# A value product moved in front of the last tile of an output projection, in a gated attention and feed-forward block

## The chip, the cores and the metric

The kernel runs on one core of one Trainium2 chip. The metric is the device time of one execution in microseconds. A core has five engines that run side by side, each through its own instructions in their order: PE (TensorE, matrix products; its weight loads are shown apart as PEld), DVE (VectorE), ACT (ScalarE), POOL (GpSimd) and SP (SyncE, which here issues almost all DMAs). Engines wait for one another by semaphores.

## The reference

There are 32 sequences of 64 tokens with 512 features, as queries (`x`) and as context (`ctx_4096`), 32 heads of width 128, and after the attention a linear layer with adapters (LoRA):

```python
q = (layernorm(x) @ Wq).reshape(b, 64, 32, 128)          # b = 32
k = (ctx @ Wk).reshape(...);  v = (ctx @ Wv).reshape(...)
score = einsum('bqhd,bkhd->bhqk', q, k) / sqrt(128) + position_bias
probs = softmax(where(mask, score, -inf)), 0 where masked
a = einsum('bhqk,bkhd->bqhd', probs, v).reshape(b, 64, 4096) @ Wo
x = x + tanh(g_xattn) * a
y = layernorm(x) @ weight.T + bias + lora(layernorm(x))
out = x + tanh(g_ffn) * y
```

All is float32. The wide products are made as three products of rounded parts: a number is split into a high part (rounded to a type that PE reads at full rate) and a low part (the rest), and high x high, high x low and low x high are summed (`mm3`). So each operand of a wide product must first be split: ACT copies it with rounding (high part), then DVE or POOL subtracts (low part).

## The kernel before

The 2048 tokens are done in two halves of 1024 tokens (`p` = 0, 1), each of which is 8 tiles of 128 tokens (`NT` = 8). A half first makes all keys and values and stores them in HBM (`stage_a`), then runs the attention (`run` within `attention`), by 16 pairs of heads (`NPR` = 16); after the second half the linear layer follows.

For one pair `n` the attention has four kinds of work on PE:
- `q_unit(n)`: the queries of the pair, 42 wide matmuls (128x512).
- `score(n, ...)`: per head 16 small matmuls of queries with keys (each stands twice in the record). Two pairs are scored at a time, 128 matmuls in the record. Behind each of the four score tiles come, on DVE, scale and bias (L863) and the row maximum (L865), then on POOL the subtraction of the maximum (L866), then a beat; ACT's exponential follows.
- `pv(n)`: the product of probabilities with values, 64 small matmuls (128 in the record) into four PSUM banks (`po`, L1010). Each bank is then rounded: ACT copies it into `ch` (L1014), DVE subtracts for `cl` (L1015), and a beat follows. There is one `ch` and one `cl`, used by almost all pairs. At its end `pv(n)` issues the load of the values of the next pair.
- `oproj(n)`: the output projection of the pair, 8 tiles of 6 wide matmuls (`mm3` of `ch`, `cl` and the weight `wo`, high and low), each added to the running sum `acc` by DVE (L1059), with a beat.

The order of PE is written out by hand. From the fifth pair on the loop of `run` goes in cycles of two pairs:

```python
for a in range(4, NPR, 2):
    oproj(a - 3)
    q_unit(a)
    start_o(a - 2)
    pv(a - 2)
    q_unit(a + 1)
    if a < NPR - 2:
        oproj(a - 2)
    start_o(a - 1)
    if a < NPR - 2:
        pv(a - 1)
    ...
    score(a, a + 1)
```

Side work is kept in a list of generators, `streams`. A call of `beat()` advances every one of them by one step, in the order of the list, and the step's instructions go to the queues of their engines at that point. `drain` runs one to its end. Among the side streams: the making of query weights (`prep`, 8 steps on ACT and POOL), the turning of probabilities (`turned`, with ACT copies L896), the bias and mask (`bias_mask`, POOL L815), and the rounding of the output weight.

That last one is `prep_o(n)`, which `start_o(n)` puts into the list. Its first step rounds one half of `wo` (ACT copies the high part, L90; POOL subtracts for the low part, L91), its second step the other half, its third issues the fetch of the next raw `wo` on SP (L259). It writes the one buffer that the projection before it has read. `oproj(n)` takes it from there; within a tile of `mm3` the first matmul reads high half 0 of `wo`, the second low half 0, the third high half 0, the fourth high half 1, the fifth low half 1, the sixth high half 1.

PSUM has eight banks, taken in turn: a projection takes 8, a value product 4, two pairs of scores 4.

## Time and profile before

| | |
|---|---|
| Median of 3 runs | 1477.29 us (1476.85 to 1477.81) |
| Profiled execution | 1477.5 us, of which 1475.7 us from the first to the last instruction (span) |
| PE | 1467.0 us busy, 99% |
| POOL | 1052.0 us, 71% |
| DVE | 940.2 us, 64% |
| ACT | 714.6 us, 48% |
| Mean granted clock of PE | 1.000 |
| Projection, wide matmuls with `ch` (L100) | 896, 278.2 us |
| Value product `po` (L1010) | 3840, 63.4 us |
| Scores `ps` (L861) | 2048, 65.2 us |
| Low half of `wo` on POOL (L91) | 56, mean 1299 ns |
| Score subtraction on POOL (L866) | 64, mean 1050 ns |

How to read it: busy times of different engines overlap and don't add up to the span. Matmuls are pipelined, their durations overlap too, so the distance from start to start counts: six wide matmuls take 1.36 us. In the chain of work that ended last PE has 97%. A line of a timeline gives the start, the duration of a group, engine, line, operation with its output and inputs, the count, and in brackets the idle time before it and what ended it.

### The profile page before, as it was taken

Reading aid. Unit: us, or ns where it says so; the run is one execution under the profiler, and the core shown is the slowest. Engines: PE = TensorE matmul, PEld = TensorE weight load, DVE = VectorE, ACT = ScalarE, POOL = GpSimd, SP = SyncE. Lnnn points to the kernel's source line nnn. Section 1 sums busy time; section 2 is a strip of 40 time slices with the busy share of each in tenths; the row PEclk is TensorE's granted clock in tenths of the full one; section 3 lists DMA queues with packets and bytes.
Section 4 is the critical chain, followed back from the end, with each engine's and each line's share of the span. In section 5 each row is a group of like instructions: output and inputs, shape, how many; then the busy total and the mean of one; then the engine's idle time right before and its main releaser. Section 6 shows DMA issues by size and latency. Waiting matters only on the chain.

```text
span 1475.7 us, 31292 instructions
## 1 busy us (share of the span) xinstructions
PE 1467.0 (99%) x12008; PEld 1220.4 (83%) x12008; DVE 940.2 (64%) x1589; ACT 714.6 (48%) x1582; POOL 1052.0 (71%) x1160
## 2 busy tenths in 40 slices
PE   9999999999999999999999999999999999999999
PEld 7888888888888888888888888888888888888887
DVE  5675464367675677576479756435767567757774
ACT  5444233346555665666334423334655665566611
POOL 4999378969767676767989938896875758577520
PEclk9999999999999999999999999999999999999999
DMA  5754554475443455353385765437545344625554
GB/s 194 287 204 164 179 179 174 143 261 185 152 168 106 168 180 208 101 186 109 127 294 203 235 226 186 173 136 260 184 152 178 103 170 170 217 93 184 136 127 131
DMA packets 148343, 259.38 MB, mean 176 GB/s; under 512 B 44417, under 2 KB 78209, under 8 KB 144098
## 3 DMA queue, kind: packets, MB, share of 16 engines
q1 hardware_dynamic: 147906, 256.87, 50.7%
q8 instruction: 94, 1.54, 0.4%
q10 hardware_dynamic: 288, 0.52, 0.1%
q14 instruction: 55, 0.45, 0.1%
HBM read 179.74 MB, written 77.61 MB: 174 GB/s over the span
## 4 chain that ended last, share of the span: by engine, by line
PE 97%; DVE 1%; issue 1%; ACT 1%; POOL 0%; DMA 0%; SPq 0%; DVEq 0%; POOLq 0%
PE pa L100 23%; PE pxq L100 6%; PE pvq L100 6%; PE pvv L100 6%; PE pxv L100 6%; PE pzv L100 6%; PE pzq L100 6%; PE pzk L100 6%; PE pvk L100 6%; PE pxk L100 6%; PE po L1010 4%; PE ps L861 4%; PE pf L100 3%; PE pyq L100 3%; PE pyv L100 3%; PE pyk L100 3%
## 5 line engine op out<-in xcount | busy, mean ns | idle before, releaser
L100 PE MATMUL pa<-wo,ch 128*128 128x512 f32 x896 | 278.2, 392 | 0.4 <-ACT ch L1014 0.4
L896 ACT COPY pt<-tp 32x256 f32<-32x256 f32 x452 | 182.4, 404 | 69.7 <-DVE tp L899 60.1
L100 PEld LDWEIGHTS pa<-wo,ch 128*128 128x128 f32 x896 | 166.6, 188 | 36.0 <-ACT ch L1014 0.7
L100 PE MATMUL pa<-wo,cl 128*128 128x512 f32 x448 | 174.1, 389 | 0.0
L1059 DVE TENSOR_TENSOR acc<-pa,acc 128x512 f32<-128x512 f32 x192 | 129.4, 681 | 53.5 <-PE pa L100 53.5
L815 POOL TENSOR_TENSOR sm<-sm,madd 128x512 f32<-128x512 f32 x60 | 77.2, 1295 | 96.5 <-DMA sm<-bias 96.5
L888 POOL TENSOR_TENSOR sm<-sm,r 128x512 f32<-128x512 f32 x64 | 66.8, 1044 | 72.5 <-DVE r L887 70.2
L351 DVE TENSOR_TENSOR vt<-pvv,vt 128x512 f32<-128x512 f32 x64 | 44.2, 691 | 103.1 <-PE pvv L100 103.1
L1015 DVE TENSOR_TENSOR cl<-po,ch 128x512 fp32r<-128x512 f32 x112 | 74.5, 689 | 47.6 <-ACT ch L1014 47.2
L100 PEld LDWEIGHTS pa<-wo,cl 128*128 128x128 f32 x448 | 84.1, 188 | 17.7
L866 POOL TENSOR_TENSOR sm<-sm,mx 128x512 f32<-128x512 f32 x64 | 67.0, 1050 | 34.9 <-DVE mx L865 34.7
L351 DVE TENSOR_TENSOR qT<-pvq,qT 128x512 f32<-128x512 f32 x64 | 44.1, 690 | 61.9 <-PE pvq L100 60.5
L373 ACT COPY vt<-pxv 128x512 f32<-128x512 f32 x32 | 18.8, 588 | 130.9 <-PE pxv L100 130.9
L875 ACT ACTIVATE sm<-sm 128x512 f32<-128x512 f32 x62 | 39.2, 633 | 78.0 <-POOL sm L866 78.0
L351 DVE TENSOR_TENSOR kT<-pvk,kT 128x512 f32<-128x512 f32 x60 | 41.1, 684 | 54.8 <-PE pvk L100 53.9
L91 POOL TENSOR_TENSOR wo<-rawo,wo 128x512 fp32r<-128x512 f32 x56 | 71.4, 1299 | 3.1 <-ACT wo L90 3.1
L1010 PEld LDWEIGHTS po<-pt,v 64*64 64x64 f32 x3840 | 59.2, 135 | 10.8 <-issue 9.3
L187 POOL TENSOR_TENSOR vs<-wvr,wvr 128x512 f32<-128x512 f32 x24 | 32.1, 1348 | 49.3 <-DMA wvr<-wv 49.3
L861 PE MATMUL ps<-kB,qT 128*64 128x64 f32 x2048 | 65.2, 223 | 2.1 <-issue 2.0
L1014 ACT CAST ch<-po 128x512 fp32r<-128x512 f32 x112 | 63.0, 594 | 7.9 <-PE po L1010 7.8
L861 PEld LDWEIGHTS ps<-kB,qT 128*64 128x64 f32 x2048 | 61.9, 138 | 5.8 <-issue 4.2
L351 DVE TENSOR_TENSOR vt<-pzv,vt 128x512 f32<-128x512 f32 x64 | 44.2, 690 | 34.0 <-PE pzv L100 33.6
(999 smaller groups left out, 3899.2 us busy)
## 6 DMA issues: line engine op xcount, KB each, us to landing
kd<-kT SPq DMA_DIRECT2D x64, 512.0 KB, 3.8
vd<-vt SPq DMA_DIRECT2D x128, 256.0 KB, 2.4
kB<-kd SPq DMA_DIRECT2D x32, 1024.0 KB, 10.6
v<-vd SPq DMA_DIRECT2D x32, 1024.0 KB, 8.0
rawq<-wq SPq DMA_DIRECT2D x32, 512.0 KB, 3.7
sm<-bias SPq DMA_DIRECT2D x64, 256.0 KB, 5.4
rawo<-wo SPq DMA_DIRECT2D x32, 512.0 KB, 3.7
rawk<-wk SPq DMA_DIRECT2D x31, 512.0 KB, 5.3
```

The source lines that it names most:

```text
L91: eng.tensor_tensor(lo, raw, hi.bitcast(F32), ALU.subtract)
L100: nc.tensor.matmul(ps, a, b, start=start and i == 0, stop=stop and i == len(todo) - 1, skip_group_check=True)
L351: nc.vector.tensor_tensor(o, ps, i, ALU.add)
L815: nc.gpsimd.tensor_tensor(t, t, masks[p][0], ALU.add)
L861: nc.tensor.matmul(ps[h * S:(h + 1) * S, t, :], qT[:, i, tok], kT[:, i, tok], start=True, stop=True)
L866: nc.gpsimd.tensor_tensor(s, s, mx.unsqueeze(2).to_broadcast([P, NT, S]), ALU.subtract)
L888: nc.gpsimd.tensor_tensor(t, t, r.unsqueeze(2).to_broadcast([P, NT, S]), ALU.mult)
L896: f(pts[n == NPR - 2][dst, i, :, qi * 32:(qi + 1) * 32], of[src, :, ki * 32:(ki + 1) * 32])
L1010: nc.tensor.matmul(ps[h][d:d + S, k, :], v[keys, t, i * P + d:i * P + d + S], pt[keys, i, t, :], start=True, stop=True)
L1014: nc.scalar.copy(o, ps[h])
L1015: nc.vector.tensor_tensor(l, ps[h], o.bitcast(F32), ALU.subtract)
L1059: nc.vector.tensor_tensor(acc[t], ps, acc[t], ALU.add)
```

## The change

In the cycles with a < NPR - 2 (a = 4, 6, 8, 10, 12, in both halves) the matmuls of `pv(a - 1)` are issued before the last tile of `oproj(a - 2)` instead of after it. Since the last tile still reads `ch` and `cl`, the four roundings of the product, each with its beat, are collected in a list and issued behind that tile. `start_o(a - 1)`, which stood between the projection and the product, now stands behind the roundings. The other calls of `pv` and `oproj` are as before.

```diff
-        def pv(n, cs=(0, 1)):
+        def pv(n, cs=(0, 1), later=None):
             drain(b["s", n])
...
                 for h in range(2):
                     o, l = [x[:, i].rearrange("p (t h s) -> p h t s", h=2, s=S)[:, h, ts[0]:ts[-1] + 1] for x in (hi, lo)]
-                    nc.scalar.copy(o, ps[h])
-                    nc.vector.tensor_tensor(l, ps[h], o.bitcast(F32), ALU.subtract)
-                    beat()
+
+                    def rounded(o=o, l=l, ps=ps[h]):
+                        nc.scalar.copy(o, ps)
+                        nc.vector.tensor_tensor(l, ps, o.bitcast(F32), ALU.subtract)
+                        beat()
+                    if later is None:
+                        rounded()
+                    else:
+                        later.append(rounded)
...
-        def oproj(n, ts=range(NT)):
+        def oproj(n, ts=range(NT), between=None):
             drain(ob.get(n))
             for t in ts:
+                if between and t == NT - 1:
+                    between()
                 ps = psum(f"pa{p}_{n}_{t}")
...
                 if a < NPR - 2:
-                    oproj(a - 2)
+                    later = []
+                    oproj(a - 2, between=lambda: pv(a - 1, later=later))
+                    for x in later:
+                        x()
                 start_o(a - 1)
-                if a < NPR - 2:
-                    pv(a - 1)
-                else:
+                if a == NPR - 2:
                     drain(b["s", a - 1])
                     next(ob[a - 1])
                     held = list(streams)
```

## The prediction

> **What bounds the kernel now.** I read the page's busy shares first, then the waits of PE (TensorE), then the order of time around the moved work, engine by engine.

> ```profile
> PE 1467.0 (99%) x12008; PEld 1220.4 (83%) x12008; DVE 940.2 (64%) x1589; ACT 714.6 (48%) x1582; POOL 1052.0 (71%) x1160
> ```

> PE is idle for 1475.7 - 1467.0 = 8.7 us in all. Its waits by name add up to about 5 us:

> ```profile
> PE ps L861 <- issue: 2.0, 4, 0.8
> PE warm L514 <- POOL ident masks.py:199: 1.3, 1, 1.3
> PE pa L100 <- DVE cx L1015: 1.1, 2, 0.8
> ```

> So no rearrangement can save more than 8.7 us (0.6%), while anything PE must newly wait for is paid in full. The question is what PE's order needs from the other engines after the move. The timelines of PE, DVE, ACT and POOL at the first of the ten changed places (a = 4, first half) answer it. Columns: start us, duration us, engine, line, operation.

> ```profile
> 418.92 0.39 PE L100 MATMUL pa<-wo,cl 128*128 128x512 f32 x1
> 419.23 2.13 PE L1010 MATMUL po<-pt,v 64*64 64x64 f32 x128
> 421.29 3.95 PE L861 MATMUL ps<-kB,qT 128*64 128x64 f32 x128
> 425.17 0.73 PE L100 MATMUL pa<-wo,ch 128*128 128x512 f32 x2
> 425.74 0.40 PE L100 MATMUL pa<-wo,cl 128*128 128x512 f32 x1
> 425.98 0.62 PE L100 MATMUL pa<-wo,ch 128*128 128x512 f32 x2
> ```
> ```profile
> 419.34 0.69 DVE L1059 TENSOR_TENSOR acc<-pa,acc 128x512 f32<-128x512 f32 x1 [0.67 <-PE pa L100]
> ...
> 423.12 1.29 DVE L1015 TENSOR_TENSOR cl<-po,ch 128x512 fp32r<-128x512 f32 x2 [0.31 <-ACT ch L1014]
> 424.32 0.68 DVE L863 SCALAR_TENSOR_TENSOR sm<-ps,sm 128x512 f32<-128x512 f32 x1
> 425.04 0.69 DVE L865 TENSOR_REDUCE mx<-sm 128x8 f32<-128x512 f32 x1
> 425.64 0.68 DVE L863 SCALAR_TENSOR_TENSOR sm<-ps,sm 128x512 f32<-128x512 f32 x1
> ```
> ```profile
> 422.50 0.74 POOL L294 TENSOR_TENSOR wq6p<-wsq,wq6p 128x256 fp32r<-128x256 f32 x1
> 423.19 2.53 POOL L91 TENSOR_TENSOR wo<-rawo,wo 128x512 fp32r<-128x512 f32 x2
> 425.80 1.04 POOL L866 TENSOR_TENSOR sm<-sm,mx 128x512 f32<-128x512 f32 x1
> 427.12 1.05 POOL L866 TENSOR_TENSOR sm<-sm,mx 128x512 f32<-128x512 f32 x1 [0.28 <-DVE mx L865]
> ```

> See POOL. The two low halves of the next output weight (L91, wo) run before the first score's subtraction (L866), and end at 425.72. The projection that reads them starts at 425.17: its second matmul (about 425.50) takes low half 0, its fifth (425.98 + 0.23 = 426.21) low half 1. The slack today is 0.5 us.

> **The change part by part, at this place; ten such places (a = 4, 6, 8, 10, 12 in two halves).**

> *PE order.* Nothing is added; tile 7 of the projection changes places with the value product. A tile repeats every 1.36 us, so the product starts at 419.23 - 1.36 = 417.87. Before a wide product it takes 2.03 (the other product of the cycle, 360.30 to 362.33). The first six wide matmuls behind it take 1.49 instead of 1.36 (362.33 to 363.82), and the step from wide matmuls to scores costs 0.09 more than wide to wide (370.62 to 372.07 = 1.45). Scores then start at 417.87 + 2.03 + 1.49 + 0.09 = 421.48, 0.19 later than now, and the next projection could start at 425.36.

> *Operands of the product, earlier by 1.36 us.* Values: issued at 402.65, landing at most 10.9 us later (slowest of 32), so 413.5. Probabilities: last turned copy on ACT at about 409.9. Both in time: 0. PSUM: the four product banks are held over tile 7, but the fourth score is the first to reuse one, at about 424.4, and that is read out by 422.9: 0.

> *Roundings.* All four pairs come behind tile 7, because tile 7 reads the very ch and cl that they overwrite. DVE first has tile 7's add, at 421.58 (scores start + 0.1) instead of 419.34, then four subtractions at a pitch of 0.60 (1.29 - 0.69): 422.18 to 423.98, then the first score's operation at 424.58, 0.26 later than now. ACT's four copies at a pitch of 0.49 (two in 1.08, one 0.59) stay ahead of that. cl is complete by 424.7, before 425.36: hidden under the scores, 0.

> *The weight rounding, which moves without being named.* The call that queues the rounding of wo as a side stream (start_o) stood before the value product, whose four beats issued both halves and the next fetch. Now it stands behind the four delayed roundings, so the four beats of the scores issue it. A beat comes after each score's POOL subtraction. POOL's queue becomes: subtraction 0, low half 0, subtraction 1, low half 1, subtractions 2 and 3. Subtraction 0 cannot start before DVE has the first row maximum: 1.48 after the score's first DVE operation (424.32 to 425.80; at another place 1126.67 to 1128.15, with POOL idle before it), so 424.58 + 1.48 = 426.06. One subtraction holds POOL 1.09 (two in 2.13, one 1.04), one half 1.24 (2.53 - 1.29):
> - low half 0: 427.15 to 428.44 (1.29 long)
> - subtraction 1: later of 424.58 + 1.32 + 1.48 = 427.38 (score pitch 425.64 - 424.32) and 427.15 + 1.24 = 428.39
> - low half 1: 429.48 to 430.77

> The high halves (ACT, 0.62 each) run right behind the ch copies and before the exponentials; ready by 424.8: 0.

> PE's second matmul therefore waits from about 425.69 to 428.44 (2.75 us), three more run, and the fifth, due at 425.36 + 1.04 = 426.40, waits to 430.77. Late: 4.37 us. With the 0.19 of reordering 4.56 per place, 45.6 in ten.

> *DMAs.* SP's queue gets the fetch of the following wo behind low half 1 instead of at 425.75, about 5 us later, and two key loads behind it (426.91 now); PE itself is 4.5 later, and these are read 20 and 49 us on: 0. The value load no longer stands behind that fetch; nobody waits for it.

> *Given back.* The score stage has gaps of issue at three of the ten places (0.37, 0.68, 0.77) and is longer by 0.26 and 0.23 at two (4.21, 4.18 against 3.95). A gap in the scores is now hidden, since low half 1 ends last: -2.3.

> *Sum.* 45.6 - 2.3 = 43.3 on the profiled execution's 1477.5 us: 1520.8. That execution stands 0.2 over the median of the three runs (1477.29), so 1521 either way.

> *Bounds.* Whether a wait is for half a tile or all of it: at the second place the projection starts at 475.09 while POOL's two halves last until 475.92, so it is by halves; if by the whole tile, PE waits with its first matmul and loses the 1.04 of overlap, +10 in all. Restart of PE after a wait: none to one weight load (0.19) at two waits, 0 to +4; I take 0, since the rows of PEld lie beside matmuls: a weight can be loaded while the matmul waits. DVE's rounding chain 0.3 shorter or longer: -3 to +3.

> *The clock.* A new wait of 2.75 us has no like in the running kernel; the longest is 1.3, at the start. The end of the trace has one:

> ```profile
> 1472.00:1473.00 1.00, 0.52 (x5) 0.31 (x3) 0.44 (x1) 0.00 (x0) 0.00 (x0) 1.00 0.39 131
> ...
> 1475.30:1475.70 0.40, 0.00 (x0) 0.00 (x0) 0.00 (x0) 0.00 (x0) 0.00 (x0) 0.59 0.00 0
> ```

> The seventh number is the granted clock. PE's last matmul ends at 1472.52 and the clock is down 2.8 to 3.2 us later. So the wait is just at the edge. Bounds: nothing, or half speed for some 2.8 us at all ten, 1.4 each, +14. I take nothing, as PE works 0.7 us between its two waits.

> [...]

> **The rivals.**
> 1. *No stall (0.05): 1477.* If the weight rounding still came ahead of subtraction 0, PE would lose only 0.19 x 10 = 1.9, and 2.3 of gaps might close. For it: POOL's backlog ends at 423.19, with 2.9 us free until 426.06, room for both halves. Against: the beats are where they are, and POOL's rows follow the order of issue.
> 2. *Half a stall (0.09): 1498.* One beat falls between, so low half 0 is ahead of subtraction 0 and low half 1 behind it, ready at 427.15 + 1.29 = 428.44: 2.04 late, 2.23 a place, 22.3 - 2.3 = +20.
> 3. *Faster (0.03): 1474.* Today 256 small matmuls follow each other and the sequencer falls behind; a wide tile between them lets it catch up. It decides from both low halves being ready before 426.40, and needs 0.5 us a place, which the issue gaps (2.0 us in all) do not hold.
> 4. *The clock drops too (0.13): 1530 to 1540,* with the wait for the whole tile in the same region.

> **How the numbers follow.** Forecast 0.70: 1521, by its own bounds 1515 to 1531. Rivals 1 and 3 are left out below (0.08), and part of rival 2; above, rival 4 up to 1538. Range 1503 to 1538. A measurement of this kernel tells about 0.2% (3 us) from no change. Faster 0.03; within 0.2% 0.05 (rival 1); slower 0.92.

> **What would show it.** PE busy stays near 1467 and its idle grows by some 43 us, put down to POOL wo L91, twenty waits of about 2.7 and 1.6 us at ten places. POOL's order reads L866, L91, L866, L91. The product starts one tile earlier with no wait; the first score's DVE operation comes about 3.1 us after the scores start. Wrong if POOL shows both L91 before L866 (rival 1), if PE waits for ch or cl, or if the granted clock falls below 1.00 in these stretches.

## The result and the profile after

The changed kernel takes 1540.95 us (median of four runs, 1539.90 to 1541.78), the kernel before beside it 1477.07 us: a ratio of 1.0427, interval 1.0415 to 1.0439, +63.9 us. It is slower, as forecast, but 3 us above the top of the range (1538), and the loss is 64 us where 44 were forecast. The profiled execution took 1541.78 us with a span of 1540.0 us, against 1477.5 and 1475.7.

First the busy share of PE on the page of the changed kernel, then its waits (us in total, times, longest):

```profile
PE 1497.4 (97%) x12008; PEld 1235.4 (80%) x12008; DVE 943.4 (61%) x1589; ACT 714.4 (46%) x1582; POOL 1050.0 (68%) x1160
```
```profile
PE pa L100 <- POOL wo L91: 35.2, 20, 2.5
PE pa L100 <- DVE cx L1017: 1.6, 2, 0.8
```

The new wait is the one forecast: twenty times for the low halves of `wo`, two at each of ten places. But it explains only part of the 64 us, and PE's busy time has grown by 30 us with the same 12008 matmuls. The timelines of POOL and of PE at the first place (a = 4, first half) show both:

```profile
426.58 1.04 POOL L866 TENSOR_TENSOR sm<-sm,mx 128x512 f32<-128x512 f32 x1 [4.30 <-DVE mx L865]
427.58 1.27 POOL L91 TENSOR_TENSOR wo<-rawo,wo 128x512 fp32r<-128x512 f32 x1
428.81 1.05 POOL L866 TENSOR_TENSOR sm<-sm,mx 128x512 f32<-128x512 f32 x1
429.81 1.27 POOL L91 TENSOR_TENSOR wo<-rawo,wo 128x512 fp32r<-128x512 f32 x1
```
```profile
418.36 2.11 PE L1010 MATMUL po<-pt,v 64*64 64x64 f32 x128
420.40 0.73 PE L100 MATMUL pa<-wo,ch 128*128 128x512 f32 x2
...
421.99 3.95 PE L861 MATMUL ps<-kB,qT 128*64 128x64 f32 x128
425.87 0.50 PE L100 MATMUL pa<-wo,ch 128*128 128x512 f32 x1
428.90 0.50 PE L100 MATMUL pa<-wo,ch 128*128 128x512 f32 x1 [2.53 <-POOL wo L91]
429.24 0.40 PE L100 MATMUL pa<-wo,cl 128*128 128x512 f32 x1
429.47 0.40 PE L100 MATMUL pa<-wo,ch 128*128 128x512 f32 x1
431.14 0.79 PE L100 MATMUL pa<-wo,ch 128*128 128x512 f32 x1 [1.27 <-POOL wo L91]
431.73 0.63 PE L100 MATMUL pa<-wo,cl 128*128 128x512 f32 x1
432.15 1.05 PE L100 MATMUL pa<-wo,ch 128*128 128x512 f32 x2
...
437.79 0.39 PE L100 MATMUL pa<-wo,cl 128*128 128x512 f32 x1
438.01 0.61 PE L100 MATMUL pa<-wo,ch 128*128 128x512 f32 x2
438.47 0.39 PE L100 MATMUL pa<-wo,cl 128*128 128x512 f32 x1
```

POOL does subtraction, half, subtraction, half; before the first subtraction it stood idle for 4.30 us, in which both halves (2.53 us in the profile before) would have had room. PE's fifth matmul starts at 431.14 instead of 425.87 + 1.04 = 426.91, 4.23 us late. And then the matmuls are slow: three wide matmuls take 1.28 us (432.15 to 433.43 from group to group), against 0.68 further down (437.79 to 438.47). The table by stretches shows the clock beside it; its columns are the stretch, its length, the busy time of PE, PEld, DVE, ACT, POOL, then the granted clock, the share of the DMA engines and GB/s:

```profile
427.13:430.54 3.41, 0.96 (x3) 0.49 (x3) 3.25 (x5) 1.26 (x2) 3.41 (x4) 1.00 0.02 7
430.54:433.95 3.41, 2.81 (x7) 2.23 (x8) 0.69 (x1) 1.26 (x2) 2.54 (x3) 0.50 0.50 181
433.95:437.36 3.41, 3.41 (x10) 2.64 (x9) 1.65 (x4) 0.00 (x0) 0.54 (x1) 0.50 1.02 429
437.36:440.77 3.41, 3.41 (x17) 2.81 (x16) 3.19 (x7) 0.22 (x1) 1.55 (x2) 1.00 0.38 159
```

The clock of PE is halved from 430.54 to 437.36. In the trace's clock records this happens at all ten places, seven times for 6.83 us and three times for 3.41 us, 58.0 us in all.

The stage sums of the two profiled executions close the account. From the first matmul of the projection to the next query unit the ten places take 174.1 us instead of 110.4 (+63.7); the ten score stages before it take 38.8 instead of 41.9 (-3.1, the gaps of issue are gone); the prediction costed the reordering at +1.9. That is 62.5 of the 64.3 us between the spans.

### The profile page after: what moved, and what is told of

Same layout as the page of the kernel before. It is cut to its first block, busy times and chain, and to the rows that moved or that the text cites. A ratio compares the mean times of both kernels' runs of the same rounds, so it can differ in the third digit from the quotient of the medians.

```text
span 1540.0 us, 31252 instructions
## 1 busy us (share of the span) xinstructions
PE 1497.4 (97%) x12008; PEld 1235.4 (80%) x12008; DVE 943.4 (61%) x1589; ACT 714.4 (46%) x1582; POOL 1050.0 (68%) x1160
## 4 chain that ended last, share of the span: by engine, by line
PE 81%; POOL 9%; issue 5%; DMA 2%; DVE 1%; ACT 1%; POOLq 0%; DVEq 0%
PE pa L100 18%; PE pzv L100 6%; PE pvv L100 6%; PE pxv L100 6%; PE pzk L100 5%; PE pvk L100 5%; PE pxk L100 5%; PE pxq L100 5%; PE pzq L100 5%; PE pvq L100 5%; PE pf L100 3%; PE pyv L100 3%; PE pyk L100 3%; PE pyq L100 2%; POOL wo L91 2%
## 5 line engine op out<-in xcount | busy, mean ns | idle before, releaser
L100 PE MATMUL pa<-wo,ch 128*128 128x512 f32 x896 | 302.2, 416 | 35.6 <-POOL wo L91 35.2
L100 PEld LDWEIGHTS pa<-wo,ch 128*128 128x128 f32 x896 | 177.6, 200 | 83.1 <-POOL wo L91 43.8
L100 PE MATMUL pa<-wo,cl 128*128 128x512 f32 x448 | 182.9, 409 | 0.0
L866 POOL TENSOR_TENSOR sm<-sm,mx 128x512 f32<-128x512 f32 x64 | 66.4, 1044 | 76.6 <-DVE mx L865 76.6
L100 PEld LDWEIGHTS pa<-wo,cl 128*128 128x128 f32 x448 | 90.1, 201 | 18.7
L91 POOL TENSOR_TENSOR wo<-rawo,wo 128x512 fp32r<-128x512 f32 x56 | 71.5, 1291 | 2.8 <-ACT wo L90 2.8
L1010 PEld LDWEIGHTS po<-pt,v 64*64 64x64 f32 x3840 | 59.0, 135 | 10.6 <-issue 9.2
L861 PEld LDWEIGHTS ps<-kB,qT 128*64 128x64 f32 x2048 | 61.2, 138 | 5.9 <-issue 5.1
L351 DVE TENSOR_TENSOR qT<-pzq,qT 128x512 f32<-128x512 f32 x64 | 44.2, 690 | 32.3 <-PE pzq L100 30.7
```

Of the source, the lines that this page charges most:

```text
L91: eng.tensor_tensor(lo, raw, hi.bitcast(F32), ALU.subtract)
L100: nc.tensor.matmul(ps, a, b, start=start and i == 0, stop=stop and i == len(todo) - 1, skip_group_check=True)
L351: nc.vector.tensor_tensor(o, ps, i, ALU.add)
L861: nc.tensor.matmul(ps[h * S:(h + 1) * S, t, :], qT[:, i, tok], kT[:, i, tok], start=True, stop=True)
L866: nc.gpsimd.tensor_tensor(s, s, mx.unsqueeze(2).to_broadcast([P, NT, S]), ALU.subtract)
L1010: nc.tensor.matmul(ps[h][d:d + S, k, :], v[keys, t, i * P + d:i * P + d + S], pt[keys, i, t, :], start=True, stop=True)
```

## The experiments

The theory after this reading, A: the place of `start_o` is the whole cause; it queues the halves of `wo` behind score subtractions, PE waits, and the wait makes the clock fall. The rivals: B, the moved product and its delayed roundings of `ch` and `cl` cost the time; C, the clock falls for a reason other than idle time.

**e1, the weight queued first.** Undoes one part of the change:

```diff
                     oproj(a - 2, between=lambda: pv(a - 1, later=later))
+                    start_o(a - 1)
                     for x in later:
                         x()
-                start_o(a - 1)
+                else:
+                    start_o(a - 1)
```

> The changed kernel with one line moved: start_o(a - 1) stands before the delayed roundings, so their four beats issue the rounding of wo, as before the change; the product stays in front of tile 7. Theory A (the loss comes from the place of start_o alone: both low halves of wo come behind score subtractions on POOL, PE waits some 4.2 us at ten places, and its clock halves after each): no waits for POOL wo, granted clock 1.00 throughout, 1475 to 1480 us. Theory B (the loss comes from the moved product and its delayed roundings of ch and cl): stays near 1541 us.

Measured: 1478.99 us, before 1479.14; ratio 0.9999 (0.9990 to 1.0008). PE no longer waits for `wo`, and its mean granted clock is 1.0 in all eleven runs. On POOL of this kernel the halves are back in front, in the idle time:

```profile
420.15 0.72 POOL L294 TENSOR_TENSOR wq6p<-wsq,wq6p 128x256 fp32r<-128x256 f32 x1
422.68 2.53 POOL L91 TENSOR_TENSOR wo<-rawo,wo 128x512 fp32r<-128x512 f32 x2 [1.80 <-ACT wo L90]
426.81 1.04 POOL L866 TENSOR_TENSOR sm<-sm,mx 128x512 f32<-128x512 f32 x1 [1.61 <-DVE mx L865]
```

So the named part of the change, the product in front of the last tile with its roundings behind, costs and brings nothing that can be measured. All ten score stages here take 3.88 or 3.89 us from their first matmul to the projection's, without the gaps of before. That is 3.1 us less in ten, and the seams of the reordering, costed at 1.9, take most of it back; the rest is within the interval. B falls.

**e2, the weight queued late, nothing else.** The other part alone, on the kernel before:

```diff
-                start_o(a - 1)
                 if a < NPR - 2:
                     pv(a - 1)
-                else:
+                start_o(a - 1)
+                if a == NPR - 2:
```

> The kernel before with one line moved: start_o(a - 1) stands behind pv(a - 1) and its roundings; the product stays behind tile 7. Theory A: POOL's order becomes subtraction, low half, subtraction, low half; PE late by about 3.5 us at ten places (35 us), and 10 to 25 us more if the clock falls: 1510 to 1537 us. Theory B: 1477 us, nothing waits.

Measured: 1521.50 us, ratio 1.0281 (1.0261 to 1.0300). The waits of PE in this kernel, and POOL's order at the first place:

```profile
PE pa L100 <- POOL wo L91: 24.8, 20, 1.7
```
```profile
425.34 1.04 POOL L866 TENSOR_TENSOR sm<-sm,mx 128x512 f32<-128x512 f32 x1 [3.48 <-DVE mx L865]
426.34 1.27 POOL L91 TENSOR_TENSOR wo<-rawo,wo 128x512 fp32r<-128x512 f32 x1
427.57 1.04 POOL L866 TENSOR_TENSOR sm<-sm,mx 128x512 f32<-128x512 f32 x1
428.58 1.27 POOL L91 TENSOR_TENSOR wo<-rawo,wo 128x512 fp32r<-128x512 f32 x1
```

At the first place the fifth matmul starts at 429.89 instead of 426.67, 3.22 late. The clock fell at eight places, 30.7 us in all. A holds: a moved line with no arithmetic of its own makes most of the loss (42 of 64 us). It is less than in the changed kernel: subtraction 0 starts 3.72 us after the scores start (421.62 to 425.34) instead of 4.59 (421.99 to 426.58). That DVE has tile 7's sum and all four roundings still before it there, and here only the later roundings, is the likely reason, but was not tried by itself.

**e3, one half first.** Half of the cause: after the delayed roundings the first step of the rounding of `wo` is issued by hand.

```diff
                 start_o(a - 1)
+                if a < NPR - 2:
+                    next(ob[a - 1])
```

> The changed kernel with the first step of the rounding of wo issued ahead of the scores (one step by hand behind start_o), the second behind the first score subtraction. Theory A: only the fifth matmul waits, for about 2.0 us at ten places: 1496 to 1500 us if the clock holds over a wait of 2 us, 1510 to 1522 us if it falls there too. Theory B: near 1541 us.

Measured: 1503.29 us, ratio 1.0161 (1.0147 to 1.0175), +24.2. One wait is left at each place:

```profile
PE pa L100 <- POOL wo L91: 18.3, 10, 1.8
```

The wait is close to what was expected, 1.83 us for about 2.0; the time lies between the two expected ranges, because the clock neither held nor fell throughout: it fell at three of ten places, for 3.41 us each. A wait of the same 1.83 us left the clock alone at seven places and was followed by a halved clock at three. Here are two stretches of the grid of 3.41 us that e5 describes, each with such a wait; after the first the clock stayed, after the second it fell. PE's busy time, 1.58 us, is the same in both, so these two are not told apart by that number:

```profile
582.56:585.97 3.41, 1.58 (x7) 1.31 (x8) 3.31 (x7) 1.23 (x2) 3.41 (x4) 1.00 0.22 50
633.76:637.17 3.41, 1.58 (x7) 1.01 (x6) 3.31 (x6) 0.83 (x2) 3.41 (x4) 1.00 0.23 42
```

**e4, the wait filled with work.** Takes away the idle time and leaves the lateness. Ahead of `oproj(a - 3)` at the ten places (in the loop's passes with a > 4) stands `fill(a, 11)`:

```diff
+            def fill(a, k):
+                drain(ob.get(a - 3))
+                px = psum(f"fill{p}_{a}")
+                for _ in range(k):
+                    nc.tensor.matmul(px, xq["p1"][0][0][:, 0:P], xq["p1"][0][0], start=True, stop=True,
+                                     skip_group_check=True)
```

> The changed kernel with eleven extra wide matmuls (2.5 us of work whose result nobody reads) ahead of the next projection at each of the ten places, where PE would wait for low half 0. If the halved clock comes from PE's idle time (theory A), the clock stays at 1.00 and more work takes less time: 1513 to 1520 us, with PE still waiting for low half 1 and projection starts at the same distance from the scores. If the clock falls for another reason (rival: the order of small and wide matmuls, or the total load), the time stays at 1541 us or grows.

Measured: 1524.13 us, ratio 1.0299 (1.0284 to 1.0315). PE does 110 matmuls more and the kernel is 17 us faster than the changed one. That is the way theory A expected, but 4 us above its range; where these 4 us come from was not traced. In its timeline and its stretches at the first place:

```profile
421.74 3.95 PE L861 MATMUL ps<-kB,qT 128*64 128x64 f32 x128
425.62 2.81 PE L1152 MATMUL fill<-x0p 128*128 128x512 f32 x11
...
430.91 0.50 PE L100 MATMUL pa<-wo,ch 128*128 128x512 f32 x1 [1.25 <-POOL wo L91]
431.25 0.40 PE L100 MATMUL pa<-wo,cl 128*128 128x512 f32 x1
```
```profile
429.53:432.94 3.41, 2.16 (x10) 1.70 (x10) 1.36 (x2) 1.31 (x3) 3.33 (x4) 1.00 0.30 90
```

The fifth matmul starts 9.17 us after the scores, 9.15 in the changed kernel: the lateness is untouched. The clock stays at 1.00 through all ten places (mean 1.0 in all four runs). So the pure lateness is worth +45.0 us (against the kernel before in the same comparison), and the halved clock the rest, 63.9 - 45.0 = 18.9 us. The traces agree within a few us: from the start of the scores to the next query unit the ten places take 152.3 us in the kernel before, 192.8 here and 213.0 in the changed kernel, that is 40.5 for the lateness and 20.2 for the clock. C falls.

**e5, the wait filled by half.** The same with `fill(a, 6)`. By now the clock records gave something finer to test: the starts of all halved stretches of the changed kernel lie on one grid of 3.413 us (430.54, 485.15, 543.18 and so on are 16 and 17 steps apart), and the step ahead of a fall held 0.95 to 1.53 us of PE work there, up to 1.75 in e2 (1150.44 to 1153.85).

> As the filled wait, with six extra matmuls (1.36 us) instead of eleven. The wait itself should end at the same point, so a time of 1524 us without the clock. Theory of the grid (the clock is set anew every 3.41 us on a fixed grid, and falls where PE idled for more than about half of that stretch): the two waits leave some 1.2 and 1.3 us with 0.7 us of work between them, so only places where both lie in one stretch fall, some four or five of ten: 1529 to 1536 us. Rival (only one wait of over 2 us in a piece makes the clock fall): no place falls, 1524 us.

Measured: 1530.24 us, ratio 1.0353 (1.0336 to 1.0371). The time lies in the range expected from the grid, and the clock fell at five of ten places. Two places of this kernel, each with the stretches in which its two waits lie and what followed; after the first the clock halved, at the second it stayed:

```profile
480.21:483.62 3.41, 1.54 (x6) 0.62 (x4) 3.19 (x5) 1.26 (x2) 3.41 (x4) 1.00 0.02 5
483.62:487.03 3.41, 2.88 (x7) 2.30 (x8) 0.69 (x1) 1.26 (x2) 2.48 (x3) 0.50 0.56 184
...
1207.24:1210.66 3.42, 2.28 (x10) 1.42 (x8) 3.35 (x6) 0.63 (x1) 3.05 (x3) 1.00 0.20 78
1210.66:1214.07 3.41, 2.15 (x10) 1.60 (x9) 1.49 (x3) 1.26 (x2) 3.41 (x4) 1.00 0.27 65
1214.07:1217.48 3.41, 3.41 (x16) 2.82 (x16) 3.05 (x7) 0.63 (x1) 1.09 (x2) 1.00 1.03 425
```

The two places and their waits (1.14 and 1.26 us at both) are of the same make; only how they lie on the grid differs. No wait in this kernel is longer than 1.3 us, so the rival (one long wait) falls.

**e6, the weight queued late, the wait filled.** e2 with `fill(a, 6)`.

> The kernel before with the rounding of wo queued late (1521.5 us before), and six extra matmuls (1.36 us) ahead of the next projection at the ten places. Theory: the wait of PE ends at the same point, the clock stays at 1.00; what is left is the pure delay of the two low halves, 3.2 us at ten places: 1508 to 1513 us. Rival (the clock falls for another reason than idle time): 1521 us or more.

Measured: 1513.25 us, ratio 1.0235 (1.0219 to 1.0252), a quarter of a us above what was expected. The clock did not stay: it fell at two places, for 6.8 us in all, which at half clock costs some 3.4 (an estimate). These are the only two places where the fill was too short: the scores ran there almost without gaps of issue (3.88 and 3.94 us), the projection came early, and PE waited for low half 0 as well (0.29 and 0.23 us) before it waited for low half 1 (1.27 and 1.26); at the other eight it waited for low half 1 alone. The direction holds (e2 less the fallen clock), the size of the rest, about 31 to 35 us, only roughly.

None of these kernels beats the one before. With PE 99% busy there and 8.7 us idle, e1 shows where this rearrangement ends: at the same time.

## Why the prediction was right and wrong

- **The weight rounding** was right, and it is the cause: e1 and e2 separate it from the rest. The sum gave 9.29 us from the start of the scores to the end of low half 1 (421.48 to 430.77); PE started on it after 9.15 us. Per place 4.37 late were forecast, 4.23 measured at the first; over all, 43.3 us were forecast against +45.0 in e4, where the clock stayed up.
- **PE order** was right: scores start 3.63 us after the product (418.36 to 421.99), 3.61 forecast. At these places PE shows no wait for the product's operands or banks; in e1 the reordering as a whole, with what is given back, comes to nothing within 1.5 us.
- **What is given back** was right in sign and roughly in size (3.1 us, 2.3 forecast), but not in its reason, so the nearness is luck. The gaps in the scores were to be hidden behind low half 1; they are gone. With tile 7 between the two runs of small matmuls every one of the ten score stages takes 3.88 us, in e1 too, where nothing hides a gap; in e2, with the product behind tile 7, the ten take 43.1 us.
- **The roundings** were right: the first score's DVE operation comes 3.11 us after the scores start, 3.10 forecast, with ACT's four copies starting already during tile 7 (421.22). Hidden, as put.
- **The clock** is the step that failed. It read "I take nothing, as PE works 0.7 us between its two waits". Measured, the clock halved at all ten places and took 18.9 us, so PE's busy time, which was to stay near 1467 us, rose to 1497. The row it was read from, the end of the trace with the clock down 2.8 to 3.2 us after the last matmul, was taken as the length of a wait that must be exceeded in one piece. In e5 no wait was longer than 1.3 us, and the clock fell at five places. In the changed kernel the 0.7 us of work between the two waits did not keep it up: the grid stretches ahead of its ten falls held 0.95 to 1.53 us of PE work. The end of the trace before goes with that: its last full stretch, 1471.96 to 1475.37, held 0.56 us, and from 1475.37 on the clock was 0.51.
- **The bounds** followed from that. Rival 4 had this outcome at a chance of 0.13 and a price of 14 us, with one halved stretch at each place; it came true at 18.9, with two stretches at seven of the ten, and 1521 + 18.9 is 1540. No run shows the 17 us by which the top of the range, 1538, stands above 1521; the runs showed these 18.9 in its place. The forecast's own lower bound, 1515, does not come out of the bounds listed: 3 us below 1521 is 1518.
- **Rivals 1, 2 and 3** fell: there is no cover (twenty waits), no half stall (e3 shows what that would have been, 1503 against 1498 forecast, part of it the clock), and no gain. Rival 3's mechanism, a wide tile that closes the gaps between the small matmuls, did take place, but is worth only those 3.1 us.

## What to carry to other kernels

Where side work is issued by the beats of the main work, moving a call past the beats moves that work in the queue of every engine it uses: list what each queue looks like afterwards, and find the first instruction in it that waits for the bottleneck engine. An idle time put into a bottleneck TensorE had two prices here, the wait itself and the clock after it, which added nearly half of the lateness again (18.9 on 45.0 us by the medians, 20.2 on 40.5 by the stages). Extra matmuls in the wait showed the second part and won it back here: 1524.13 us in e4 against 1540.95.

## What the hardware showed that was not expected

| Profile | Falls | PE work in the step ahead of a fall, us | Steps with a wait and no fall, us |
|---|---|---|---|
| Changed kernel | 10 | 0.95 to 1.53 | 2.28 and more |
| e2 | 8 | up to 1.75 | 1.90 and more |
| e3 | 3 | 1.58 in each | 1.58, 1.72 and more |
| e4 | 0 | none | 2.15 and more |
| e5 | 5 | up to 1.71 | 1.94, 2.02 and more |
| e6 | 2 | 1.85 and 1.93 | 2.15 and more |

These are counts; no run varied the work in a step by itself, and 1.58 stands on both sides in e3. In the 28 falls of these profiles the clock stayed down for a second step where PE's work in the first was 2.19 to 2.81 us, and came back after one where it was 2.88 us (e5) or more; no run varied that by itself either. In the halved stretches of the changed kernel's first place six wide matmuls took 2.56 us (432.15 to 434.71), 0.427 each, against 1.36, 0.227 each, at full clock.
